# Expert adapters multiplied in the unused columns of the score banks, half of the products parked in DRAM

## The chip, the core and the metric

The kernel runs on one core of one Trainium2 chip. The metric is the device time of one execution in microseconds (us). The kernel before took 2158.56 us, the median of three runs (2157.76 to 2160.24). A difference is spoken of as such from 0.2% on.

## What is computed

Two transformer layers with normalisation after each block, over 8 batches of 512 tokens of width 512, all in float32. What matters here is the first layer: causal attention with 16 heads of 32, then a mixture of 8 experts of which each token uses two. Every expert's weights carry a low-rank adapter (rank R = 16, scale 2):

```python
gup = jnp.einsum('th,eho->teo', xf, gate_up_proj)
gup = gup + SCALING * jnp.einsum('ter,eor->teo', jnp.einsum('th,erh->ter', xf, gup_lora_A), gup_lora_B)
...
out = jnp.einsum('tei,eih->teh', h, down_proj)
out = out + SCALING * jnp.einsum('ter,ehr->teh', jnp.einsum('tei,eri->ter', h, down_lora_A), down_lora_B)
```

The kernel multiplies each adapter out once (A times B, a full 512 x 512 or 256 x 512 matrix) and adds it to the expert's weights, so that the tokens see merged weights. That is 8 experts x 6 chunks of 128 x 512.

## The kernel before

**Stages.** `attention0` (L1231) does the first attention for batches b = 0 to 7. Within a batch it goes over four groups of four heads, g = 0 to 3, and in each over three units u of score blocks (`UNITS`, L1239): u = 0 is key block 0, u = 1 is key blocks 1 and 3, u = 2 is key block 2, whose scores are 256 columns wide. The experts' tiles of 128 tokens follow (`Tiles.step`, L954), then the second attention and the feed-forward layer, which the change does not touch.

**A unit.** `scores` (L1392) takes the tile `sc`, four PSUM banks of 512 columns, one bank for each head of the group; the pool `p_sc` has one such buffer. Each score matmul is cut into two of 64 columns (`matmul_by_columns`, L58), and the four heads lie on four different groups of 32 rows, so that eight matmuls stand side by side in the array. ScalarE takes the exponential of all four banks (L1403), GpSimd masks the diagonal (L1408). For u = 2 only columns 0 to 255 of each bank are used. After the scores come the thunks that `plan(b)` (L1453) has put into the slot `todo[g, u]` (projections, queries, keys, values, routing), then the product of the unit before (L1413), and at u = 1 the row sums of the group before (L1434), whose inverse goes through the two `r_inv` buffers.

**The adapters.** `merge` (L1447) handles one chunk of two experts: two matmuls with 16 rows and 128 columns each into two buffers of the pool `p_mm` (which has two, and serves all projections), two multiplications by 2 on ScalarE into `r_inv` buffers (L800), two additions into the weights on GpSimd (L802). Twelve of the 24 merges lie in batches 1 to 6, two in each, in the slots (2, 2) and (3, 2) behind the batch's key or ahead of its `score`. The other twelve, for experts 4 to 7, come after the last attention group: their weights can be loaded only once the memory of the attention weights is free (`room`, L768). They are spread over `tiles.step` 0 to 10, one in each (L1552 to L1585). Tile 12 is the first that uses an expert from 4 on.

**Who sets the order.** Up to batch 7, g = 2, and for the other engines up to L1586, a scheduler orders each engine's instructions by its own estimate of times; from there on TensorE keeps the order of the source (`in_order`, L65, L1532). SyncE (SP) issues nearly all DMAs from one queue, in order: loads, the `results` of the tiles (L936), the normalised rows (L195). GpSimd (POOL) issues the gathers of token rows (L850) and does the two small operations of each layer normalisation (L189, L190), in one queue with its additions.

**Around the end of the attention.** Step 0 of the tiles, then batch 7's output projection (L1558 to L1562), whose four tiles VectorE adds and takes statistics of (L1336, L187, L188). GpSimd makes the reciprocal deviation (L189, L190), VectorE normalises (L192), and behind that in VectorE's queue lie the routing table (L597, L598) and the hidden product of the next tile (L913), which TensorE turns in `turn_hidden` (L919).

Of the kernel before, what the change touches and what calls it, by code (L numbers as in the profile page):

```python
# [9 lines left out]
F32 = mybir.dt.float32  # L10
# [4 lines left out]
ALU = mybir.AluOpType  # L15
# [3 lines left out]
P = 128  # L19
NB = 8  # L20
S = 512
# [3 lines left out]
E = 8  # L25
R = 16
NHID = 1408 // P
UPS = 6
# [3 lines left out]
LORA_SCALE = 2.0  # L32
# [14 lines left out]
EXPERT = UPS * 512  # L47
# [10 lines left out]
def matmul_by_columns(nc, out, lhsT, rhs, start=True, stop=True, columns=32):  # L58

    for at in range(0, P, columns):  # L60
        m = slice(at, at + columns)
        nc.tensor.matmul(out[m], lhsT=lhsT[:, m], rhs=rhs, start=start, stop=stop)  # L62
# [8 lines left out]
class Inputs:  # L71
# [3 lines left out]
    def __init__(self, *aps):  # L75
        for name, ap in zip(self.names, aps, strict=True):
            setattr(self, name, ap)
# [156 lines left out]
def lora_factors(lo, c):  # L234

    if c < ND:
        return lo[:, ts(c, P)], lo[:, 512:1024]
    return lo[:, 1536 + P * (c - ND) : 1536 + P * (c - ND + 1)], lo[:, 1024:1536]
# [520 lines left out]
class Experts:  # L759

    def __init__(self, env, pool):
        self.env, self.nc = env, env.nc
        self.w = pool.tile([P, E * EXPERT], F32, name="experts")
        self.by_expert = self.w.rearrange("p (e f) -> p e f", f=EXPERT)

# [15 lines left out]
        for j in range(4):  # L783
            self.nc.sync.dma_start(out=self.lora[32 * j : 32 * j + R, :], in_=self.env.ins.lora[i, j])

    def delta(self, ps, e, c):
        j = 32 * (e % 4)
        a, bt = lora_factors(self.lora[j : j + R, :], c)
        self.nc.tensor.matmul(ps, lhsT=a, rhs=bt, start=True, stop=True)

    def chunk(self, e, c, n=1):
        return self.by_expert[:, e : e + n, 512 * c : 512 * (c + 1)]

    def merge(self, e, c, ps, scaled):


        for i in range(2):
            self.delta(ps[i], e + i, c)
        for i in range(2):
            self.nc.scalar.mul(scaled[i], ps[i], LORA_SCALE)  # L800
            w = self.chunk(e + i, c)[:, 0, :]
            self.nc.gpsimd.tensor_tensor(w, w, scaled[i], ALU.add)  # L802


class Tiles:
# [425 lines left out]
def attention0(env, guard, keep, routes, experts, dram, p_mm, tiles_ctx):  # L1231
# [4 lines left out]
    tc, nc, ins, xs, vec = env.tc, env.nc, env.ins, env.xs, env.vec  # L1236
# [3 lines left out]
    with ExitStack() as phase:  # L1240
# [22 lines left out]
        def load_x(b):  # L1263
            xs[b] = work.tile([P, NT, D], F32, tag="x", name=f"x_{b}", bufs=2)
            nc.sync.dma_start(out=xs[b], in_=ins.x[b].rearrange("(t p) d -> p t d", p=P))
# [30 lines left out]
        def mm(shape, name):  # L1296
            return p_mm.tile(shape, F32, tag="mm", name=name)
# [94 lines left out]
        def scores(b, g, u):  # L1392
            q, k = heads[b, g]
            sc = p_sc.tile([P, 4, S], F32, tag="sc", name="sc")
            width = 0
            for kt in UNITS[u]:
                w = S - P * kt
                for j in range(4):
                    hs = slice(HD * j, HD * (j + 1))
                    matmul_by_columns(nc, sc[:, j, width : width + w], k[hs, ts(kt, P)], q[hs, P * kt :], columns=64)  # L1400
                width += w
            p = own.tile([P, 4, width], F32, tag=f"p{u}", name="p", bufs=2 if u == 0 else 1)
            nc.scalar.activation(p, sc[:, :, :width], AF.Exp, scale=scale)  # L1403

            at = 0
            for kt in UNITS[u]:
                first = p[:, :, at : at + P]
                nc.gpsimd.affine_select(out=first, in_=first, pattern=[[0, 4], [1, P]], compare_op=ALU.is_ge, fill=0.0,  # L1408
                                        base=0, channel_multiplier=-1)
                at += S - P * kt  # L1410
            return p
# [30 lines left out]
            nc.vector.tensor_tensor(aoTs[b][:, g, :], av, r_inv, ALU.mult)  # L1442
            guard.watch_inverses(r_inv)

        merges = [(e, c) for e in range(0, E, 2) for c in range(UPS)]

        def merge(n=1):  # L1447
            for _ in range(min(n, len(merges))):
                e, c = merges.pop(0)
                ps = [mm([P, 512], "ps_lora") for _ in range(2)]  # L1450
                experts.merge(e, c, ps, [work.tile([P, 512], F32, tag="r_inv", name="scaled", bufs=2) for _ in ps])

        def plan(b):  # L1453

            todo, late = ({(g, u): [] for g in range(ND) for u in range(len(UNITS))} for _ in range(2))
            for slot, places in (((0, 0), (0, 1)), ((0, 1), (3,)), ((0, 2), (2,))):
                todo[slot] += [lambda t=t: value(b, t) for t in places]
            pb, last = b - 1, b == NB - 1
            by_dma = 0 <= pb < by_blocks
            for g in range(ND):  # L1460
                nb, ng = (b, g + 1) if g + 1 < ND else (b + 1, 0)
                if nb < NB:
                    todo[g, 0 if by_dma and ng == 0 else 1].append(lambda nb=nb, ng=ng: query(nb, ng))
                    todo[g, 1 if by_dma and ng == 0 else 2].append(lambda nb=nb, ng=ng: key(nb, ng))
            if b:
                places = ((1, 0), (1, 1), (1, 2), (2, 0)) if by_dma else ((1, 0), (1, 0), (1, 1), (1, 1) if last else (1, 2))
                for t, slot in enumerate(places):
                    todo[slot].append(lambda t=t: project(pb, t))
                if by_dma:
                    todo[2, 1].append(lambda: blocks(pb))  # L1470
                else:
                    for c in range(ND):
                        at = todo[2, 1] if last and c >= 2 else (late if last else todo)[2, 0]
                        at.insert(c % 2 if at is todo[2, 1] else len(at), lambda c=c: turn(pb, c))
                todo[(3, 2) if by_dma else (2, 1)].append(lambda: score(pb))
                if not by_dma:
                    todo[2, 2].append(lambda: choose(pb))
                if not last:
                    todo[2, 2 if by_dma else 1].append(merge)
                    todo[3, 2 if by_dma else 1].insert(0, merge)  # L1480
            if b == 0:
                todo[1, 0].append(lambda: router.merge_lora(mm([P, ND, E], "ps_wr")))
            if b > 1:
                todo[0, 0].append(lambda: choose(b - 2))
                todo[1, 0].append(lambda: dispatch(b - 2))
                todo[1, 2].append(lambda: enter(one_hot(b - 2, range(NT))))
            if last:
                todo[1, 2].append(soon)
                todo[2, 2].append(first_rows)
                late[3, 1].append(first_turned)  # L1490
                todo[3, 2] += [begin, lambda: dispatch(b - 1)]
            return todo, late
# [25 lines left out]
        for b in range(NB):  # L1518
            todo, late = plan(b)
            for g in range(ND):  # L1520
                if g == 2:
                    if b + 1 < NB:
                        load_xT(b + 1)

                    nc.gpsimd.tensor_tensor(xs[b], xs[b], row[:, 1:2, :].to_broadcast([P, NT, D]), ALU.add)
                if g == 3 and b + 1 < NB:
                    load_x(b + 1)
                if b == NB - 1 and g == 1:
                    experts.load_lora(work, 1)
                    experts.load(4)  # L1530
                if b == NB - 1 and g == 2:
                    order.enter_context(in_order(tc))  # L1532
                if b == NB - 1 and g == 3:
                    experts.load(5)
                    experts.load(6)
                acc = []
                for u in range(len(UNITS)):
                    p = scores(b, g, u)
                    for thunk in todo[g, u]:
                        thunk()  # L1540
                    begun.close()
                    if waiting is not None:
                        waiting()
                    for thunk in late[g, u]:
                        thunk()
                    if u == 1 and summing is not None:
                        summing()
                    waiting = lambda b=b, g=g, u=u, p=p, acc=acc: product(b, g, u, p, acc)
                summing = lambda b=b, g=g, acc=acc: normalise(b, g, acc)
# [6 lines left out]
        b = NB - 1  # L1556
# [321 lines left out]
def usual_pass(tc, ins, held_out):  # L1878
    nc = tc.nc
    with ExitStack() as ctx:  # L1880
        env = Env(ctx, tc, ins)
# [3 lines left out]
        with tc.tile_pool(name="a_mm", bufs=2, space=PSUM) as p_mm, ExitStack() as attn1_ctx:  # L1885
            with tc.tile_pool(name="routes", bufs=1, side="right") as routes, \
                    tc.tile_pool(name="experts", bufs=1, side="right") as pool, ExitStack() as tiles_ctx:
                experts = Experts(env, pool)
                router, tiles, tables = attention0(env, guard, keep, routes, experts, dram, p_mm, tiles_ctx)

                def load_rows(b):
# [335 lines left out]
```

## Time and profile before

| what | us |
|---|---|
| median of three runs | 2158.56 |
| the profiled execution, its own time | 2158.07 |
| its span on the core | 2156.4 |
| outside the span (2158.07 less 2156.4) | 1.67 |
| TensorE busy | 2121.3 |
| window 148 to 235 (about one batch): TensorE, VectorE, ScalarE, GpSimd busy | 86.57, 60.76, 27.97, 29.84 |
| window 690 to 810 (end of the attention, first tiles): the same | 118.33, 62.34, 32.66, 50.69 |

TensorE's busy time counts matmuls from their start to a modelled end, and matmuls that overlap once. Since a 512-column matmul's modelled end lies past the start of the next, the price of a group of matmuls is best taken from start to start: the time from its first start to the start of the next group. In the timeline, the columns are the start in us, the duration, the engine, the source line, the operation with output, inputs, array tile (rows*columns) and operand shape, how many records are merged, and in brackets the idle time before with what ended it. A float32 matmul leaves two records.

### The profile page before, as it was taken

To read this page: it belongs to the slowest core of one execution; us is meant where nothing else is said; L and a number is where in the kernel's file an instruction comes from. 1 tells how busy PE (TensorE), PEld (TensorE's weight loads), DVE (VectorE), ACT (ScalarE), POOL (GpSimd) and SP (SyncE) were. 2 spreads that over 40 slices of the span, in tenths; PEclk is the share of its full clock that TensorE was granted. 3 is DMA by queue.
4 is the path that set the end of the run, shared out by engine and by line. 5 is a ranking of instruction groups with operands and counts; after the bars stand their busy time and mean duration, and the time that the engine had idled before them with its cause. 6 is when DMAs were issued, how large, how long until landed. Compare 5 with 4: busy or idle time off the path is not lost. (4 is left out here: it accounts for less than half of the span.)

```text
span 2156.4 us, 35260 instructions
## 1 busy us (share of the span) xinstructions
PE 2121.3 (98%) x14746; PEld 996.3 (46%) x14746; DVE 1280.0 (59%) x2042; ACT 628.8 (29%) x907; POOL 495.0 (23%) x489
## 2 busy tenths in 40 slices
PE   9999999999998999999999999999999999999997
PEld 2333333333333444444443333333334888888886
DVE  2657676776767544224326988889857644555443
ACT  2332323323323221122124333332332232222222
POOL 2333414424233342132014222232211000000000
PEclk9999999999999999999999999999999999999999
DMA  9030312303222228797644121331201311111000
GB/s 308 21 95 6 99 30 71 99 2 98 71 68 89 98 91 231 214 234 195 193 157 139 57 87 55 98 98 40 79 1 45 103 59 59 59 59 59 20 20 21
DMA packets 160010, 195.53 MB, mean 91 GB/s; under 512 B 61010, under 2 KB 101970, under 8 KB 157282
## 3 DMA queue, kind: packets, MB, share of 16 engines
q1 hardware_dynamic: 148560, 157.49, 23.8%
q0 software_dynamic: 10560, 34.61, 5.6%
q8 instruction: 119, 1.95, 0.4%
q10 hardware_dynamic: 722, 1.07, 0.1%
q14 instruction: 49, 0.40, 0.1%
HBM read 123.67 MB, written 69.47 MB: 90 GB/s over the span
## 5 line engine op out<-in xcount | busy, mean ns | idle before, releaser
L911 PE MATMUL ps_gu<-experts,xrT 128*128 128x512 f32 (+1 forms) x520 | 247.4, 598 | 0.0
L1403 ACT ACTIVATE p<-sc 128x2048 f32<-128x2048 f32 (+1 forms) x96 | 153.1, 1595 | 144.8 <-PE sc L62 121.1
L1165 DVE SCALAR_TENSOR_TENSOR hT<-ps_u,vec,sg 128x512 f32<-128x512 f32 x88 | 65.6, 746 | 189.4 <-PE ps_u L1160 189.4
L1176 PE MATMUL ps_f<-ffn_w,h_half 128*128 128x512 f32 x672 | 169.7, 393 | 2.7 <-DVE h_half L1171 2.0
L1015 POOL TENSOR_TENSOR g_total<-g_total,r_inv 128x512 f32<-128x512 f32 x64 | 90.0, 1406 | 352.4 <-DVE r_inv L1788 270.2
L1408 POOL TENSOR_SCALAR_AFFINE_SELECT p<-p 128x512 f32<-128x512 f32 x128 | 90.2, 717 | 341.0 <-ACT p L1403 303.5
L1431 DVE TENSOR_TENSOR p<-p 128x1536 f32<-128x1536 f32 (+2 forms) x96 | 139.3, 1451 | 44.6 <-POOL p L1408 41.2
L1758 ACT ACTIVATE p<-sc 128x1024 f32<-128x1024 f32 x128 | 124.1, 1022 | 99.0 <-PE sc L62 98.9
L913 DVE TENSOR_TENSOR h<-ps_gu,h 128x256 f32<-128x256 f32 x67 | 28.5, 425 | 207.0 <-ACT h L912 207.0
L1788 DVE RECIPROCAL r_inv<-r_inv 128x512 f32<-128x512 f32 x32 | 107.1, 3346 | 68.5 <-ACT r_inv L1012 68.5
L1176 PEld LDWEIGHTS ps_f<-ffn_w,h_half 128*128 128x128 f32 x672 | 124.4, 188 | 34.9 <-DVE h_half L1171 7.7
L1160 PE MATMUL ps_g<-x_high,ffn_w 128*128 128x512 f32 x352 | 137.2, 390 | 0.9 <-DVE x L1730 0.9
L1160 PE MATMUL ps_g<-x_low,ffn_w 128*128 128x512 f32 x352 | 137.0, 389 | 0.0
L911 PEld LDWEIGHTS ps_gu<-experts,xrT 128*128 128x128 f32 x520 | 95.6, 196 | 89.5 <-issue 89.2
L1160 PE MATMUL ps_u<-x_high,ffn_w 128*128 128x512 f32 x352 | 136.9, 389 | 0.0
L1160 PE MATMUL ps_u<-x_low,ffn_w 128*128 128x512 f32 x352 | 136.9, 389 | 0.0
L927 PE MATMUL ps_y<-experts,hT 128*128 128x512 f32 (+1 forms) x272 | 128.0, 593 | 0.5 <-ACT hT L921 0.5
L62 PE MATMUL ps_q<-experts 128*32 128x512 f32 x1024 | 121.9, 605 | 4.9 <-DMA experts<-in_xT 4.6
L62 PE MATMUL sc<-qT,kT 64*64 64x512 f32 x1024 | 124.7, 602 | 1.1 <-ACT qT L1664 0.7
L1777 PE MATMUL av<-p,v 128*64 128x512 f32 x512 | 120.9, 593 | 0.0
L62 PE MATMUL ps_o<-attn_out,aoT 128*64 128x512 f32 x512 | 116.4, 598 | 0.8 <-ACT r_inv L1012 0.8
L62 PE MATMUL ps_k<-experts 128*32 128x512 f32 x1024 | 116.3, 594 | 0.0
(269 smaller groups left out, 3275.8 us busy)
## 6 DMA issues: line engine op xcount, KB each, us to landing
results<-y SPq DMA_DIRECT2D x68, 256.0 KB, 2.2
turned<-turned SPq DMA_DIRECT2D x56, 256.0 KB, 4.1
pair<-xrT SPq DMA_DIRECT2D x25, 512.0 KB, 3.1
xrT<-pair SPq DMA_DIRECT2D x100, 128.0 KB, 4.5
x<-in_x SPq DMA_DIRECT2D x8, 1024.0 KB, 8.3
experts<-in_gate_up SPq DMA_DIRECT2D x8, 1024.0 KB, 11.4
rows<-x SPq DMA_DIRECT2D x32, 256.0 KB, 2.3
x<-rows SPq DMA_DIRECT2D x8, 1024.0 KB, 15.4
```

The source lines that it names most:

```text
L62: nc.tensor.matmul(out[m], lhsT=lhsT[:, m], rhs=rhs, start=start, stop=stop)
L911: nc.tensor.matmul(ps, lhsT=xT[:, c, :], rhs=self.weights(i, c), start=c == 0, stop=c == ND - 1)
L927: self.nc.tensor.matmul(ps, lhsT=hT[:, c, :], rhs=self.weights(i, ND + c), start=c == 0, stop=c == self.NI - 1)
L1015: self.nc.gpsimd.tensor_tensor(self.total, self.total, r_inv, ALU.add)
L1160: nc.tensor.matmul(ps, lhsT=w[:, ts(dc, P)], rhs=x[:, dc, :], start=(dc, i) == (0, 0), stop=(dc, i) == (ND - 1, 1))
L1176: self.nc.tensor.matmul(os[t], lhsT=h[:, ts(t, P)], rhs=self.weights(2 * NHID + c), start=(c, i) == (0, 0), stop=(c, i) == (NHID - 1, 1))
L1403: nc.scalar.activation(p, sc[:, :, :width], AF.Exp, scale=scale)
L1408: nc.gpsimd.affine_select(out=first, in_=first, pattern=[[0, 4], [1, P]], compare_op=ALU.is_ge, fill=0.0, base=0, channel_multiplier=-1)
L1431: nc.vector.tensor_tensor(total[:, :, P * kt :], total[:, :, P * kt :], p[:, :, at : at + w], ALU.add)
L1758: nc.scalar.activation(p, sc, AF.Exp, scale=scale)
L1777: nc.tensor.matmul(st["av"][HD * j : HD * (j + 1), :], lhsT=st["v"][:, kt, HD * j : HD * (j + 1)], rhs=p[:, j, :], start=kt == 0, stop=kt ...
L1788: nc.vector.reciprocal(r_inv, r_inv)
```

## The change

- `merge` in batches 1 to 6 and its matmuls in the tail are gone. In their place, each unit u = 2 of batches 1 to 6 (24 units) computes half a chunk, 256 columns, for four experts at once, in the free columns 256 to 511 of its own `sc` banks (`delta_halves`): four adapters on four row groups, each cut in two by 64 columns, ahead of the unit's scores.
- After the unit's exponential, ScalarE multiplies two banks at a time by 2 into two new buffers `scaled0`, `scaled1` (one of each), two multiplications in each unit (`merge_halves`).
- In batches 1 to 3 these are experts 0 to 3, and GpSimd adds them to the weights. In batches 4 to 6 they are experts 4 to 7, and SP writes them to a DRAM tensor `deltas`.
- In the tail `merge` reads the products back into the `r_inv` buffers (24 reads of 256 KB on SP) and GpSimd adds them. Its twelve places stay, without matmul and ScalarE work.
- The second set of adapters is loaded in batch 4 rather than in batch 7.
- The scratch area of GpSimd's DMA descriptors is halved (8192 bytes per partition[...]), which makes room for the two buffers.

```diff
@@ Experts
-    def __init__(self, env, pool):
+    def __init__(self, env, pool, dram):
         self.env, self.nc = env, env.nc
+        self.deltas = dram.tile([P, 4, EXPERT], F32, name="deltas")
...
-    def delta(self, ps, e, c):
-        j = 32 * (e % 4)
-        a, bt = lora_factors(self.lora[j : j + R, :], c)
-        self.nc.tensor.matmul(ps, lhsT=a, rhs=bt, start=True, stop=True)
-
-    def chunk(self, e, c, n=1):
-        return self.by_expert[:, e : e + n, 512 * c : 512 * (c + 1)]
-
-    def merge(self, e, c, ps, scaled):
-
+    def delta_halves(self, ps, c, half):
+
+        for e in range(4):
+            a, bt = lora_factors(self.lora[32 * e : 32 * e + R, :], c)
+            matmul_by_columns(self.nc, ps[:, e, :], a, bt[:, 256 * half : 256 * (half + 1)], columns=64)
+
+    def merge_halves(self, ps, second, c, half, scaled):
+
+        f = slice(512 * c + 256 * half, 512 * c + 256 * (half + 1))
+        for e, two in zip((0, 2), scaled):
+            two = two.rearrange("p (e f) -> p e f", e=2)
+            self.nc.scalar.mul(two, ps[:, e : e + 2, :], LORA_SCALE)
+            if second:
+                self.nc.sync.dma_start(out=self.deltas[:, e : e + 2, f], in_=two)
+            else:
+                w = self.by_expert[:, e : e + 2, f]
+                self.nc.gpsimd.tensor_tensor(w, w, two, ALU.add)
+
+    def merge(self, e, c, deltas):
 
         for i in range(2):
-            self.delta(ps[i], e + i, c)
-        for i in range(2):
-            self.nc.scalar.mul(scaled[i], ps[i], LORA_SCALE)
-            w = self.chunk(e + i, c)[:, 0, :]
-            self.nc.gpsimd.tensor_tensor(w, w, scaled[i], ALU.add)
+            self.nc.sync.dma_start(out=deltas[i], in_=self.deltas[:, e + i - 4, ts(c, 512)])
+            w = self.by_expert[:, e + i, ts(c, 512)]
+            self.nc.gpsimd.tensor_tensor(w, w, deltas[i], ALU.add)
@@ attention0, scores(b, g, u)
             sc = p_sc.tile([P, 4, S], F32, tag="sc", name="sc")
+            beside = halves.pop(0) if u == 2 and 0 < b < NB - 1 else None
+            if beside:
+                experts.delta_halves(sc[:, :, S - 256 :], *beside[1:])
...
             nc.scalar.activation(p, sc[:, :, :width], AF.Exp, scale=scale)
+            if beside:
+                scaled = [own.tile([P, 512], F32, tag=f"scaled{i}", name="scaled") for i in range(2)]
+                experts.merge_halves(sc[:, :, S - 256 :], *beside, scaled)
...
-        merges = [(e, c) for e in range(0, E, 2) for c in range(UPS)]
+        halves = [(second, c, half) for second in (False, True) for c in range(UPS) for half in range(2)]
+        merges = [(e, c) for e in range(4, E, 2) for c in range(UPS)]
 
         def merge(n=1):
             for _ in range(min(n, len(merges))):
                 e, c = merges.pop(0)
-                ps = [mm([P, 512], "ps_lora") for _ in range(2)]
-                experts.merge(e, c, ps, [work.tile([P, 512], F32, tag="r_inv", name="scaled", bufs=2) for _ in ps])
+                experts.merge(e, c, [work.tile([P, 512], F32, tag="r_inv", name="delta", bufs=2) for _ in range(2)])
@@ plan(b)
-                if not last:
-                    todo[2, 2 if by_dma else 1].append(merge)
-                    todo[3, 2 if by_dma else 1].insert(0, merge)
@@ the loop over b and g
+                if b == NB // 2 and g == 0:
+                    experts.load_lora(work, 1)
                 if b == NB - 1 and g == 1:
-                    experts.load_lora(work, 1)
                     experts.load(4)
@@ kernel
-    nc = bacc.Bacc("TRN2", target_bir_lowering=False, num_devices=1)
+    nc = bacc.Bacc("TRN2", target_bir_lowering=False, num_devices=1, dynamic_dma_scratch_size=8192)
```

More of the change, by code (lines that the diff above doesn't have):

```diff
@@ L1887, in usual_pass @@
                     tc.tile_pool(name="experts", bufs=1, side="right") as pool, ExitStack() as tiles_ctx:
-                experts = Experts(env, pool)
+                experts = Experts(env, pool, dram)
                 router, tiles, tables = attention0(env, guard, keep, routes, experts, dram, p_mm, tiles_ctx)
```

## The prediction

> **What bounds the kernel now.** I read the page's first part, then the timeline of TensorE in one batch and at the end of the attention, then GpSimd's and VectorE's timelines there, last the DMA issues. The first line of the page says that TensorE is the bound:
>
> ```profile
> PE 2121.3 (98%) x14746; PEld 996.3 (46%) x14746; DVE 1280.0 (59%) x2042; ACT 628.8 (29%) x907; POOL 495.0 (23%) x489
> ```
>
> So matmul time that goes is gained, unless TensorE then waits. TensorE in batch 2 (groups g = 2 and g = 3), an adapter pair amid the work:
>
> ```profile
> 231.66 3.64 PE L62 MATMUL ps_k<-experts 128*32 128x512 f32 x32
> 235.23 2.00 PE L789 MATMUL ps_lora<-lora 16*128 16x512 f32 x4
> 237.16 1.07 PE L1423 MATMUL av<-p,v 128*32 128x384 f32 x16
> ...
> 249.54 0.69 PE L62 MATMUL sc<-q,k 32*64 32x256 f32 x16
> 250.16 1.44 PE L789 MATMUL ps_lora<-lora 16*128 16x512 f32 x4
> 252.03 1.06 PE L498 MATMUL ps_logits<-x1T,r_wr 128*32 128x512 f32 x8 [0.43 <-ACT scaled L800]
> ```
>
> From start to start the first pair costs 237.16 - 235.23 = 1.93 us, the second 252.03 - 250.16 = 1.87. At the end of the attention the same pair costs less, since both `p_mm` buffers are free:
>
> ```profile
> 726.84 1.13 PE L789 MATMUL ps_lora<-lora 16*128 16x512 f32 x4
> 727.90 1.98 PE L911 MATMUL ps_gu<-experts,xrT 128*128 128x512 f32 x4
> 729.72 0.38 PE L919 MATMUL ps_hT<-ident,h 128*128 128x128 f32 x2
> ```
>
> That is 1.06 us; the batches pay about 0.85 more for waiting on a buffer. GpSimd and VectorE at the same place, where batch 7 is normalised and the next tile's hidden product follows:
>
> ```profile
> 721.12 0.23 POOL L189 TENSOR_SCALAR rstd<-mv 128x4 f32<-128x4 f32 x1 [12.40 <-DVE mv L188]
> 721.43 1.04 POOL L190 TENSOR_TENSOR rstd<-rstd,neg_half 128x4 f32<-128x4 f32 x1
> ```
> ```profile
> 722.52 1.92 DVE L192 TENSOR_SCALAR x<-x,mv,rstd 128x512 f32<-128x512 f32 x4 [1.49 <-POOL rstd L190]
> ...
> 725.21 0.42 DVE L913 TENSOR_TENSOR h<-ps_gu,h 128x256 f32<-128x256 f32 x1
> ```
>
> The reader is to see a chain: from the start of `rstd` to the end of `h` 725.63 - 721.12 = 4.5 us, and TensorE turns that `h` at 729.72, four us later.
>
> [...]eight-tile groups of 512 columns go from 219.66 to 220.70, 1.04 us, and groups of 384 and 128 one behind the other from 199.51 to 200.56, 1.05. The fixed part is paid once for groups of the same mode. [...]The trace has 2.2 for writes of that size and, for loads issued by SP with 2 KB rows, 4.3 at 512 KB.
>
> **Part 1, batches 1 to 6.** Removed: in every batch one pair of 1.93 and one of 1.87, that is 3.80. Added: four half chunks. 256 columns at the rate of a projection wave (200.56 to 204.01, 3.45 us for four waves of 512, so 0.86 each) are 0.43, and the fixed part of 0.18 is shared with the scores of the same mode that follow. Bounds: 0.43 and the stand-alone price of a 256-column group, 250.16 - 249.54 = 0.62. I take 0.43; four are 1.72.
>
> Added wait: the next group's scores need the one `sc` buffer, now free only after two more multiplications (1.08 for two, from 728.06 in ScalarE's timeline; 0.6 for one). Behind them on TensorE stands everything. For g = 0, 1 and 2 a key (3.5) and a product (1.0) lie between, which hide it; the exponential of u = 2 ends at 232.85 and the next scores start at 238.16. Without the pair those would start at 236.2, and the key's copy on ScalarE ends at 236.05, so nothing is left but also nothing lost. For g = 3 only `score` (0.88) and a product (1.0) lie between: `sc` starts at 249.97, the exponential runs from about 250.7 to 251.8, the multiplications to 252.85, the next scores could start at 253.0, TensorE would be there at 252.4. The order of the built programs shows that the scheduler puts one lone value matmul there and takes it out of the following batch of four: 0.86 for a wave of its own. Bounds 0 and 0.86; I take 0.86.
>
> Per batch -3.80 + 1.72 + 0.86 = -1.22, times six **-7.3 us** (bounds: -12.5 with the lone matmul free, -2.8 with halves at 0.62).
>
> Beside it, priced at nothing: ScalarE has eight multiplications in a batch rather than four, 2.4 us more on 28 busy of 87; GpSimd eight additions (1.5 on average) rather than four in batches 1 to 3, none in 4 to 6, on 30 of 87; SP has eight writes of 256 KB in a batch, which stand ahead of the rows and loads in its queue, but wait for ScalarE only at the end of u = 2, long before those are due. If ScalarE had no slack at g = 3, each multiplication would cost 0.6. The adapters' four loads, moved from batch 7 to SP's queue in batch 4, have two units of scores and products and three values (3.5 each) until their first use, some 15 us against the 7.4 that such a load takes to land. The halved scratch: gathers are issued 1.26 us apart and land in 4.0, so about four are in flight; nothing shows that half the room is too little. Zero; the upper bound is a gather that waits for the one before, and at 4 us each the gathers of the tiles would still keep pace with a step of 5.95.
>
> **Part 2, the tail.** Removed: twelve pairs. From start to start in TensorE's timeline: 1.99 (696.30), 1.06 (702.14), 1.06, 1.06 plus a wait of 0.15 (733.90), 1.06 of 1.87 at 744.09 (the rest waits for the logits' copy, which stays), and seven of 1.06. The sum is **13.8**. A step then takes 5.95 rather than 7.06.
>
> Added: the additions wait for reads from DRAM. In the built order GpSimd's queue is now: four gathers, addition 1, a gather, the last `g_total`, additions 2 to 12, and only then `rstd` of batch 7. Before, four additions stood ahead of it. So the normalisation waits for twelve reads, which pass through two buffers. The times, on the clock of before: the gathers start at 696.67 as now and end at 701.5; addition 1 (1.27) ends at 702.8 and frees its buffer; read 2 lands L later. From then on each buffer goes read, addition, read: L + 1.27 + 0.2 for the semaphores. Addition 2 ends at 704.3 + L, addition 4 at 705.8 + 2L, addition 12 four cycles later, at 711.7 + 6L. That is when `rstd` starts. Its input would be there at 718, so this wait is the last. The hidden product ends 4.5 us later, TensorE can turn it 0.1 after that. TensorE would be there at 729.72 - 1.99 - 1.06 - 1.06 = 725.6. The stall is 711.7 + 6L + 4.6 - 725.6 = **6L - 9.3**.
>
> L is not in the trace. Below: the 2.2 of the writes. Above: 4.3, the median of the 512 KB loads. Gathers of 256 KB take 3.5 to 4.2 with the issue on GpSimd (about 1 us) in it. I take 3.2: stall 9.9. At 2.2 it is 3.9, at 4.3 it is 16.5.
>
> What waits behind: three gathers behind additions 16, 22 and 24, not needed before steps 6 to 9, some 20 us later; expert 7's load and `results` behind the reads on SP, with two output buffers, about even with their need by the same arithmetic, 0 to 2 us; I take 0. The tail nets -13.8 + 9.9 = **-3.9**.
>
> **Sum.** -7.3 - 3.9 = -11.2, against the execution's own 2158.07 (span 2156.4 and 1.67 around it): **2146.9**. The median of the runs is 0.49 above the profiled one, nothing that matters here.
>
> **The rivals.** (a) Reads as quick as writes: the stall is 3.9 and the time 2140.9, or 2136 with the lone matmul free as well. For it: hardly any traffic at that place. Against it: no load on SP's queue has a median below 3.6 in the list of DMA issues. (b) No change: reads at 3.9 (stall 14.1, tail +0.3) and halves at 0.62 each (-2.8): 2155.6. For it: the 512 KB loads; half a chunk takes sixteen weight loads where a pair took four. (c) Slower, by one mechanism: the chain of reads and additions ahead of `rstd`. The gain is eaten at 6L - 9.3 = 7.3 + 13.8, L = 5.1; at L = 6 the stall is 26.7 and the time 2163.7. For it: loads of 256 KB at the kernel's start, amid other traffic, take 3.6 to 4.0, and five gathers and an expert's load run beside these. Against it: the DMA share in that window is 0.28. (d) That the change doesn't do what it says cannot be: the built order has all 24 groups in their places.
>
> **How the numbers follow.** Forecast 0.51 (2143 to 2152), (a) 0.22, (b) 0.16, (c) 0.11. What a measurement of this kernel can tell from no change is 0.2%, 4.3 us. Faster are the forecast and (a), 0.73; the same 0.16; slower 0.11. The range reaches from (a), 2137.5, to past (b), 2157; what is left out is (c) and a little of (a).
>
> **What would show it.** Right: groups of `sc` out of `lora` at 0.4 us each; batches 1 to 6 each 1.2 us shorter; batch 7's `rstd` idle on a DMA or on additions until about 731; a wait of TensorE for `h` of about 10 us near 726, and none later. Wrong: an L outside 2.2 to 4.3; a wait of `sc` for ScalarE in g = 0 to 2; TensorE waiting for gathers or outputs at later steps; halves at over 0.62.

## The result and the profile after

The changed kernel takes 2164.4 us (median of 10 runs, 2160.9 to 2168.0), the kernel before 2158.6 in the same comparison; the ratio is 1.0027, 95% interval 1.0018 to 1.0035. So it is slower by about 6 us, where 2146.9 was forecast. The profiled execution spans 2162.6 us against 2156.4. The page's first part shows what kind of loss that is:

```profile
PE 2106.2 (97%) x15034; PEld 995.6 (46%) x15034; DVE 1280.4 (59%) x2042; ACT 627.7 (29%) x907; POOL 488.4 (23%) x489
```

TensorE is busy 15.1 us less than before (2121.3), as the change meant it to be, and still ends 6.2 later: it now waits 21 us more, that is, stands idle for something that isn't there yet. The waits of TensorE in the kernel after (engine, operation, line, what it waited for; us in total, times, longest) name new ones (`x1T` are the turned rows that come back from DRAM for the router, `p` the masked scores, `av` their product with the values):

```profile
PE ps_logits L498 <- DMA x1T<-turned: 5.4, 3, 2.6
PE ps_rank L62 <- DVE xrT L895: 4.4, 1, 4.4
...
PE av L1437 <- POOL p L1422: 3.9, 3, 1.7
PE ps_o L1338 <- DVE x L1344: 2.7, 1, 2.7
...
PE ps_hT L927 <- DVE h L921: 2.6, 1, 2.6
```

Only the last was in the forecast. To place the loss I use two marks in TensorE's timeline that every kernel here has: the start of the last group of row sums `rs` (before: 695.30), and the stretch from it to the 67th of the 68 groups of `ps_y` that follow (before: 413.2). Up to the first mark the changed kernel loses 5.6 us (forecast -7.3); between the marks it gains 0.3 (forecast -3.9); behind them it loses 0.9.

The end of batch 2 in TensorE's timeline of the kernel after, which answers to the pair shown of before:

```profile
248.13 0.69 PE L62 MATMUL sc<-lora 16*64 16x256 f32 x16
248.61 0.64 PE L62 MATMUL sc<-q,k 32*64 32x256 f32 x16
249.18 1.07 PE L498 MATMUL ps_logits<-x1T,r_wr 128*32 128x512 f32 x8
...
251.21 1.02 PE L62 MATMUL ps_v<-experts 128*32 128x512 f32 x2
```

The half chunk and the scores together take 249.18 - 248.13 = 1.05, where the scores alone took 0.62: the half costs 0.43, as priced. The last line is the lone value matmul (a group of values that stands by itself). The batches' ends (starts of `ps_logits`) lie at 162.88, 249.18 and 335.52, before at 165.40, 252.03 and 338.56: 2.5 to 3.0 us ahead. Then it turns. Batch 4 ends at 424.62, batch 5 at 512.96, batch 6 at 602.85 (before 425.32, 513.10, 599.73), so that a lead of 3.0 has become a lag of 3.1. SyncE's timeline at the end of batch 4, first before, then after:

```profile
410.33 1.24 SPq L1265 DMA_DIRECT2D x<-in_x  x1
```
```profile
410.65 2.94 SPq L800 DMA_DIRECT2D deltas<-scaled  x2
413.69 0.46 SPq L1273 DMA_DIRECT2D x<-in_x  x1
415.01 0.33 SPq L103 DMA_DIRECT2D x1T<-turned  x1
```

Two writes of group g = 2 stand ahead of the load of `x`. On GpSimd the addition to `x` then starts late (first before, then after), with the masks of `p` behind it; on TensorE, `ps_logits` waits for `x1T` and `av` for the mask:

```profile
419.71 4.55 POOL L1525 TENSOR_TENSOR x<-x,row 128x2048 f32<-128x2048 f32 x1 [2.25 <-DMA x<-in_x]
```
```profile
422.20 4.51 POOL L1536 TENSOR_TENSOR x<-x,row 128x2048 f32<-128x2048 f32 x1 [7.74 <-DMA x1T<-turned]
```
```profile
424.62 1.07 PE L498 MATMUL ps_logits<-x1T,r_wr 128*32 128x512 f32 x8 [1.94 <-DMA x1T<-turned]
427.36 1.07 PE L1437 MATMUL av<-p,v 128*32 128x384 f32 x16 [1.67 <-POOL p L1422]
```

The table of windows says why (window, its length, busy time and instructions of TensorE, its weight loads, VectorE, ScalarE and GpSimd, then the granted clock as a share of full speed, the busy share of the DMA engines, and GB/s). Here 420 to 424, before and after:

```profile
420.00:424.00 4.00, 4.00 (x47) 1.40 (x40) 0.00 (x0) 1.66 (x4) 4.00 (x1) 1.00 0.63 242
```
```profile
420.00:424.00 4.00, 2.68 (x48) 0.85 (x40) 0.00 (x0) 2.57 (x5) 1.80 (x1) 1.00 1.00 398
```

From 408 to 420 the share was 0.91 to 0.96 already before. The mean over window 148 to 235, 0.20, hid such a stretch of some 15 us with the DMA engines nearly always busy. Before, it ends at about 422.5 (a share of 0.63 of the four us); the changed TensorE is at `ps_logits` at 424.62 - 1.94 = 422.7, so there was next to no slack for two writes more.

The third such wait, 2.58 us at 602.85, costs more than it lasts. The windows behind it show the granted clock, 0.50 in the second:

```profile
600.00:603.00 3.00, 0.42 (x20) 0.18 (x8) 0.00 (x0) 2.00 (x3) 3.00 (x1) 1.00 0.39 148
603.00:606.00 3.00, 3.00 (x24) 1.04 (x18) 1.90 (x1) 0.58 (x1) 1.65 (x3) 0.50 0.46 159
```

In finer windows the half clock lasts from 603.0 to 606.2, so 1.6 us are lost. (The kernel before has such stretches too, 682.2 to 685.7 and 747.0 to 750.4.) In the tail, the places that the forecast showed of before (GpSimd, VectorE, TensorE):

```profile
730.85 1.27 POOL L810 TENSOR_TENSOR experts<-experts,delta 128x512 f32<-128x512 f32 x1 [0.61 <-DMA delta<-deltas]
732.09 0.23 POOL L189 TENSOR_SCALAR rstd<-mv 128x4 f32<-128x4 f32 x1
```
```profile
733.49 1.92 DVE L192 TENSOR_SCALAR x<-x,mv,rstd 128x512 f32<-128x512 f32 x4 [7.08 <-POOL rstd L190]
```
```profile
736.58 0.69 PE L927 MATMUL ps_hT<-ident,h 128*128 128x128 f32 x2 [2.57 <-DVE h L921]
737.06 3.12 PE L919 MATMUL ps_gu<-experts,xrT 128*128 128x512 f32 x4
```

`rstd` starts as the twelfth addition ends, `h` is late, and behind the wait the next group takes 3.12 rather than 1.88: half clock again (0.50 from 736.2 to 739.5).

### The profile page after: what moved, and what is told of

It is laid out like the page before. It is cut to its first block, busy times and chain, and to the rows that moved or that the text cites. A ratio compares the mean times of both kernels' runs of the same rounds, so it can differ in the third digit from the quotient of the medians.

```text
span 2162.6 us, 35888 instructions
## 1 busy us (share of the span) xinstructions
PE 2106.2 (97%) x15034; PEld 995.6 (46%) x15034; DVE 1280.4 (59%) x2042; ACT 627.7 (29%) x907; POOL 488.4 (23%) x489
## 5 line engine op out<-in xcount | busy, mean ns | idle before, releaser
L1422 POOL TENSOR_SCALAR_AFFINE_SELECT p<-p 128x512 f32<-128x512 f32 x128 | 81.9, 653 | 200.1 <-ACT p L1414 196.6
L62 PE MATMUL ps_v<-experts 128*32 128x512 f32 x1024 | 121.1, 595 | 0.0
```

## The experiments

All were timed beside the kernel before, which took 2157.9 to 2159.0 in these comparisons. "Attention" is the first mark less that of before, "tail" the stretch between the marks less that of before, both from the profile of one execution. Where the tail's program is that of before it reads 0.0 to 1.7: half clock costs 1.7 us between the marks in the kernel before and in the first set only, 3.4 in the three runs that read 1.6 or 1.7. The attention of the four kernels with the writes behind the loads and four halves in each of the batches 1 to 6 is the same program, and reads -2.6 to -4.5. And the profiled execution can lie off the median of its runs (writes by ScalarE 2.9 above, both mends 2.3 above, first set only 2.3 below). So 2 us in these two columns mean little; the ratios rest on 5 to 19 runs each.

| run | us | ratio to before [95%] | attention | tail |
|---|---|---|---|---|
| the change | 2164.4 | 1.0027 [1.0018, 1.0035] | +5.6 | -0.3 |
| first set only | 2152.1 | 0.9974 [0.9965, 0.9984] | -9.7 | 0.0 |
| writes behind loads | 2154.1 | 0.9980 [0.9973, 0.9986] | -3.0 | -1.1 |
| writes by ScalarE | 2162.2 | 1.0018 [1.0010, 1.0025] | +7.6 | -1.7 |
| no round trip | 2140.3 | 0.9921 [0.9907, 0.9934] | -3.7 | -14.0 |
| no additions | 2139.9 | 0.9922 [0.9909, 0.9934] | -4.5 | -14.0 |
| GpSimd in order | 2158.5 | 1.0002 [0.9993, 1.0010] | +4.4 | -4.2 |
| both mends | 2149.5 | 0.9961 [0.9948, 0.9974] | -2.6 | -2.9 |
| scratch alone | 2157.3 | 0.9994 [0.9986, 1.0002] | -0.6 | 1.7 |
| first set, none at g = 3 | 2145.4 | 0.9943 [0.9930, 0.9957] | -15.1 | 1.7 |
| before, no tail additions | 2158.2 | 1.0002 [0.9994, 1.0010] | -0.9 | 1.6 |
| all, one at g = 3 | 2151.6 | 0.9976 [0.9968, 0.9984] | -1.9 | -6.2 |
| clear of routing | 2148.3 | 0.9952 [0.9938, 0.9965] | -2.8 | -7.6 |

**First set only.** The tail's `merge` is that of before, with matmuls and ScalarE, and the second adapters load in batch 7 again.

```diff
-            beside = halves.pop(0) if u == 2 and 0 < b < NB - 1 else None
+            beside = halves.pop(0) if u == 2 and 0 < b < NB // 2 else None
```

> One part of the change alone: experts 0 to 3 are multiplied out in the score banks in batches 1 to 3; the twelve pairs of experts 4 to 7 stay in the tail as matmuls, as before, and nothing goes through DRAM. Batches 4 to 6 then carry neither pairs nor halves. My theory (the loss of the change sits in the round trip through DRAM: writes in batches 4 to 6, reads in the tail): the attention loses 6 x 3.80 us of pairs, gains 12 halves of 0.45 and, in the three batches with halves, about 1.8 us at the start of the following batch, so -22.8 + 5.4 + 5.5 = -12; the tail is as before; 2146.5 us, between 2143 and 2151. Rival (the halves themselves, their ScalarE work and the order of GpSimd's queue cost what the pairs did): within 4 us of before, 2155 or more. Second rival (the halved scratch area slows the gathers): the tail is longer than before by several us, whatever the attention does.

Measured 2152.1, one over the range and below the rival's 2155: without DRAM the change gains. The attention gives 9.7 of the expected 12; batches 4 to 6, which have no pairs, now end on the mask (`av` waits 3.5 us for it there).

**Writes behind loads.**

```diff
-                self.nc.sync.dma_start(out=self.deltas[:, e : e + 2, f], in_=two)
+                write = lambda out=out, two=two: self.nc.sync.dma_start(out=out, in_=two)
+                write() if held is None else held.append(write)
...
+            while beside and held:
+                held.pop(0)()
```

> The changed kernel with one difference: in batches 4 to 6 the two writes of group g = 2 are issued by SP behind the load of x and the return of x1T, not ahead of them. My theory (these two writes, 2.9 us of SP's time, hold up the load of x and the return of x1T; TensorE then waits for x1T at the score and for the mask that stands behind the addition to x on GpSimd): the three waits for x1T (1.94, 0.90, 2.58 us) and most of the waits for the mask (1.67, 1.54) go, with the half clock that follows the longest (1.6); 8 to 10 us less than the changed kernel, 2155 us. Rival (it is the traffic of the writes as a whole or ScalarE's work that slows batches 4 to 6): no more than 2 us less, 2162 or more.

Measured 2154.1, 10.4 less than the change. The place of six writes, two in each of three batches, is worth 8.6 us of attention. GpSimd and TensorE at the end of batch 4 in this run:

```profile
418.84 4.56 POOL L1541 TENSOR_TENSOR x<-x,row 128x2048 f32<-128x2048 f32 x1 [4.08 <-DMA x<-in_x]
```
```profile
422.93 1.06 PE L498 MATMUL ps_logits<-x1T,r_wr 128*32 128x512 f32 x8
```

**Writes by ScalarE.**

```diff
-                self.nc.sync.dma_start(out=self.deltas[:, e : e + 2, f], in_=two)
+                self.nc.scalar.dma_start(out=self.deltas[:, e : e + 2, f], in_=two)
```

> The changed kernel with all 24 writes issued by ScalarE, at the same points of the program, so that SP's queue is as before the change and the traffic is that of the change. If SP's time for issuing is the cause (2.9 us ahead of the loads), nearly all of the 8 to 10 us comes back, less what ScalarE loses by issuing (each issue delays the logits' copy or the next exponential): 2156 to 2159. If the cause is that 512 KB of writes share the DMA engines with the loads of x, x1T and xT (3 MB), the waits for x1T stay at 1 us or more and no more than 4 us come back: 2160 to 2164.

Measured 2162.2, in the range that stood for the traffic: SyncE's 2.9 us of issuing are not the cause, and that part of my theory falls. SyncE issues the load of `x` ahead of where it did in the change (411.85 rather than 413.69), and the addition to `x` is as late as there:

```profile
422.62 4.51 POOL L1536 TENSOR_TENSOR x<-x,row 128x2048 f32<-128x2048 f32 x1 [8.41 <-DMA x1T<-turned]
```

So it made no difference to that addition which engine issued the 512 KB: it starts at 422.62, against 422.20 with SyncE's writes and 419.71 before. The DMA engines are as busy, with a share of 0.95 to 1.01 in every two us from 410 to 424.

**No round trip, and no additions.** The first leaves out writes, reads and additions. The second, on the kernel with the writes behind the loads, keeps writes and reads:

```diff
-            w = self.by_expert[:, e + i, ts(c, 512)]
-            self.nc.gpsimd.tensor_tensor(w, w, deltas[i], ALU.add)
```

> The changed kernel with the products of experts 4 to 7 computed and scaled as in the change, but neither written to DRAM nor read back nor added: the adapters of experts 4 to 7 are left out of the result. It prices the whole round trip with the twenty-four additions in the tail. My theory: attention shorter than before by about 1.3 us per batch at most (-12.4 of pairs against halves, +5.7 of lone value matmuls, +2 to +4 of waits for the value's copy): -3 to -5; tail shorter by the pairs' 13.8 less what VectorE cannot keep up with (2.7 at the output projection, 2 to 4 at the routing): -7 to -9; together 2145 to 2149. Rival (the halves and the freed tail are worth nothing even without DRAM, since VectorE and the order of the queues take it all): 2154 or more.

> The kernel with the two writes behind the loads (2154.1 us), with the products of experts 4 to 7 written and read back, but the 24 additions on GpSimd in the tail left out: the adapters of experts 4 to 7 are missing from the result. It tells the reads on SP's queue from the additions on GpSimd. My theory (the tail loses to the additions: the normalisation stands behind twelve of them, and VectorE's short operations last until a GpSimd addition beside them is over, 1.2 us where 0.2 to 0.3 are usual): the tail becomes that of the kernel without the round trip, 13 us less, 2141 us, between 2139 and 2144, and the waits of TensorE for VectorE at the output projection (3.3) and at the ranks (4.5) are gone. Rival (24 reads of 256 KB ahead of the outputs in SP's queue hold two output buffers and with them VectorE): these waits stay, 2148 or more.

Measured 2140.3 and 2139.9, the first below its range. In both the tail is shorter by 14.0, about what the pairs had cost (13.8; in part by chance, since TensorE also waits 3.5 us there, where before shows 0.2, and loses 1.7 less to half clock). So 24 reads that wait for no addition cost nothing, VectorE keeps up (I had it losing 5 to 7), and the 24 additions cost as much as the pairs. How, VectorE's and GpSimd's timelines of the change show, during the routing of batch 7:

```profile
757.21 1.27 DVE L534 SCALAR_TENSOR_TENSOR rest<-r_hots,pr 128x32 f32<-128x32 f32 x1
...
758.74 1.25 DVE L526 TENSOR_TENSOR tmp<-rest,second 128x32 f32<-128x32 f32 x1
```
```profile
757.17 1.26 POOL L810 TENSOR_TENSOR experts<-experts,delta 128x512 f32<-128x512 f32 x1 [1.16 <-DMA delta<-deltas]
758.67 1.27 POOL L810 TENSOR_TENSOR experts<-experts,delta 128x512 f32<-128x512 f32 x1 [0.24 <-DMA delta<-deltas]
```

and the same two operations without additions:

```profile
739.14 0.19 DVE L534 SCALAR_TENSOR_TENSOR rest<-r_hots,pr 128x32 f32<-128x32 f32 x1
...
739.58 0.19 DVE L526 TENSOR_TENSOR tmp<-rest,second 128x32 f32<-128x32 f32 x1
```

Each of these operations meets an addition and ends with it: the first at 758.48, its addition at 758.43, the second at 759.99, its addition at 759.94. Not every operation is held so. The reciprocal at 754.92 lies inside an addition (754.74 to 756.01) and keeps its 0.18, while the product at 755.14 lasts 0.92, to 756.06 (0.19 without additions). The rival, that the reads in SyncE's queue hold up the tiles' outputs and with them VectorE, does not fit the trace: from 754.92 to the copy that TensorE waits for (763.51) VectorE has no idle time, and between the marks it waits for an output only once, at 1077.85.

TensorE at the ranks, before, in the change with the group behind it at half clock, and without additions:

```profile
755.61 0.41 PE L62 MATMUL ps_rank<-both,r_before 128*128 128x32 f32 x2
```
```profile
764.25 0.63 PE L62 MATMUL ps_rank<-both,r_before 128*128 128x32 f32 x2 [4.39 <-DVE xrT L895]
...
765.12 3.76 PE L919 MATMUL ps_gu<-experts,xrT 128*128 128x512 f32 x4
```
```profile
743.47 0.41 PE L62 MATMUL ps_rank<-both,r_before 128*128 128x32 f32 x2 [0.94 <-DVE xrT L895]
```

**GpSimd in order, and both mends.** GpSimd keeps the program's order in the tail; the second run has the writes behind the loads as well.

```diff
         waiting()
         summing()
+        pinned = phase.enter_context(ExitStack())
+        pinned.enter_context(in_order(tc, mybir.EngineType.Pool))
         merge()
...
+        pinned.close()
         order.close()
```

> The changed kernel with GpSimd's tail kept in the order of the program from the last attention group on: four additions, not twelve, stand ahead of the reciprocal deviation of batch 7, and two additions follow in each step. My theory (the normalisation behind twelve additions costs the stall of 2.6 us at the hidden product and the half clock after it, 1.2; the other waits come from additions beside VectorE's work and stay): 3 to 5 us less than the changed kernel, 2160.5, between 2158 and 2163. Rival (the stall only moves: VectorE is the bound from the output projection on): no change, 2163.5 or more.

> Both mends together: the two writes of g = 2 behind the loads, and GpSimd's tail in the order of the program. If the two are independent: 2154.1 less 1.3 for the stall that is left there at the hidden product and what the half clock costs, 2151.5, between 2149 and 2153.5. If GpSimd's order only moves the wait: 2154 or more.

Measured 2158.5 (5.9 less than the change, within the range, though its 14 runs spread from 2154.1 to 2165.2) and 2149.5. `rstd` starts as its input arrives (idle before it 10.97, for `mv`), and the wait for `h` is gone. TensorE's waits for `x` at the output projection (1.9) and ahead of the ranks (4.8 and 5.3) stay. The run without additions shows no wait at the first place and 0.94 at the second, so I put them down to additions beside VectorE's operations.

**Scratch alone.** On the kernel before.

```diff
-    nc = bacc.Bacc("TRN2", target_bir_lowering=False, num_devices=1)
+    nc = bacc.Bacc("TRN2", target_bir_lowering=False, num_devices=1, dynamic_dma_scratch_size=8192)
```

> The kernel before with the scratch area for GpSimd's DMA descriptors halved and nothing else. My theory: no effect, 2158.4 within 1 us. Rival (gathers wait for room): more than 1 us slower.

Measured 2157.3 against 2158.3: it costs nothing that these runs could show.

**First set, none at g = 3.**

```diff
-            beside = halves.pop(0) if u == 2 and 0 < b < NB // 2 else None
+            beside = halves.pop(0) if u == 2 and g < 3 and 0 < b < 5 else None
```

> Experts 0 to 3 in the score banks as in the run with the first set only (2152.1 us), but the twelve half chunks lie in g = 0, 1 and 2 of batches 1 to 4 and none in g = 3; the pairs of experts 4 to 7 stay in the tail, nothing goes through DRAM. The built order has no lone value matmul any more. My theory (a half chunk at g = 3 costs, besides its 0.45, a value matmul of its own at 0.95 and a wait of 0.7 for the value's copy at the start of the next batch): three times 1.65 is gone, 2147, between 2144.5 and 2149.5. Rival (what TensorE saves there it waits for elsewhere, since the mask behind the addition to x ends the batch): no more than 2 us less, 2150 or more.

Measured 2145.4, 6.7 less than with three of them at g = 3, where 5 was expected, and the best of all: 12.5 us under before, 19 under the change.

**Before, no tail additions.** On the kernel before, in `merge`.

```diff
             self.nc.scalar.mul(scaled[i], ps[i], LORA_SCALE)
+            if e >= 4:
+                continue
             w = self.chunk(e + i, c)[:, 0, :]
             self.nc.gpsimd.tensor_tensor(w, w, scaled[i], ALU.add)
```

> The kernel before with the 24 additions of experts 4 to 7 in the tail left out (their matmuls and multiplications stay): these adapters are missing from the result. It asks whether the additions, which cost 14 us in the changed tail, cost something in the tail of before. My theory (VectorE waits for a GpSimd addition beside it there too, but TensorE with its pairs is the slower, except around the routing of batch 7): 0 to 2 us less than before, 2157. Rival (the additions on GpSimd are a cost of this tail at any pace): 5 us less or more, 2153 or below.

Measured 2158.2 against 2157.9: there the same additions are free. My reason, that TensorE with its pairs is slower than VectorE with its collisions, is not shown by this run. A VectorE operation beside an addition is long there too (`mine<-r_part,r_hots` at 756.84 lasts 0.93, to 757.77, where it takes 0.18 without additions), but in the trace of before the additions hardly meet the routing at all: they lie at 745.99 to 748.47 and from 756.44 on, and the two operations shown above take 0.19 each, at 750.03 and 750.48. So the place of the additions may count as much as the pace of TensorE.

**All, one at g = 3.** From both mends; writes held back go out at the next u = 2.

```diff
-            beside = halves.pop(0) if u == 2 and 0 < b < NB - 1 else None
+            at_unit = (g in (1, 2)) if b == 0 else (g < 3 or b == 6)
+            beside = halves.pop(0) if u == 2 and at_unit else None
```

> The kernel with both mends (2149.5 us) and the 24 half chunks spread over g = 1 and 2 of batch 0, g = 0 to 2 of batches 1 to 7 and one g = 3 in batch 6, so that only one lone value matmul is left. By the same theory five lone value matmuls of 0.95 and three waits of 0.7 for the value's copy go: 7 us less, 2143, if nothing else waits; the halves in batch 7 and the last write stand close to the tail's first read, which may give 1 or 2 us back: between 2142 and 2147. Rival (the mask and the loads at the batch's end take it): 2148 or more.

Measured 2151.6, a miss. From batch 1's end to batch 7's (`ps_logits` at 169.56 and 666.98, in both mends 163.83 and 667.10) it gains the expected 5.9. In the profile batch 0 takes it back: two additions (57.43 to 59.9) stand there ahead of a mask for which TensorE waits, with half clock behind it (a mean granted clock of 0.66 from 60 to 65):

```profile
60.56 1.07 PE L1442 MATMUL av<-p,v 128*32 128x256 f32 x8 [3.87 <-POOL p L1427]
```

In the sum the attention is as long as with both mends. The profiled execution lies 2.2 below the median of its runs, and why that median is 2.1 above both mends stays open; the two intervals overlap.

**Clear of routing.** From both mends; no merges in the three steps of the routing, two in each of the last steps.

```diff
         choose(b, P)
         tiles.step()
-        merge()
...
             tiles.step()
-            merge()
+            merge(2)
```

> The kernel with both mends (2149.5 us) and one more difference: the three merges that lay in the steps of batch 7's routing are taken out of those steps and done two at a time in the steps after them, so that no addition of GpSimd lies beside VectorE's routing chain. My theory ([...]the copy of the next token rows, queued behind the routing, comes late): TensorE's wait before the ranks falls from 4.8 to about 1 us, as in the kernel without additions, and the half clock after it (3 us more for the two groups that follow) goes: 6 to 7 us less, 2143, between 2141 and 2146. Rival (the wait before the ranks comes from the outputs behind the reads in SP's queue, or the weights of experts 4 to 7 now come late): no more than 2 us less, 2147.5 or more.

Measured 2148.3: 1.2 less than both mends by the medians, 1.9 by the ratios, which is the size that the rival gave. Its reason isn't what shows, though: the wait ahead of the ranks falls from 4.79 to 0.94, and the second routing table comes 7.0 us earlier (70.06 rather than 77.05 after the first mark). Of that, 4.8 are left at the second mark: with two merges to a step the additions stand ahead of gathers, for which TensorE waits at two steps (0.31, 0.75). Another 1.5 go behind the second mark, which I did not settle, and the profiled execution of both mends lies 2.3 above the median of its runs: 4.8 - 1.5 - 2.3 is 1.0, about the 1.2 of the medians.

## Why the prediction was wrong

The likeliest case and the rivals (a) and (b) were wrong; (c) came near the time (2163.7) by a mechanism that is not the one at work: its L was 6, and L is 2.45. That is luck. Of the 17.5 us between forecast and result some 12.9 lie in the attention (-7.3 against +5.6), 3.6 in the tail (-3.9 against -0.3), 0.9 behind.

**Right.** Halves at 0.43. The lone value matmul at 0.95 (priced 0.86). The removed pairs of the tail at 13.8 (14.0 when nothing takes their place, in part by chance). Zero for the scratch area. The chain through `rstd`: additions 2 and 12 start at 711.24 and 730.85, so two take 3.92, which leaves 3.92 - 1.27 = 2.65 from the end of an addition to the next one on its buffer. The read is issued 0.03 after that end (712.52 and 712.55); my 0.2 for the semaphores is an assumption that no run shows by itself, and with it L is 2.45; the formula's 711.7 + 6L gives 726.4, and `rstd` starts at 732.09 less the 5.62 by which the attention is late, 726.47. Only the size of L was off, 3.2 against 2.45; the stall by the formula is 5.4. TensorE shows 2.57 of it, because the wait for `x` ahead of it (2.74) makes TensorE itself late.

**Wrong, the step that decided.** "SP has eight writes of 256 KB in a batch, which stand ahead of the rows and loads in its queue, but wait for ScalarE only at the end of u = 2, long before those are due", priced at nothing. It asked when the loads are needed and not how busy the DMA engines were ahead of that (a share of 0.91 to 0.96 from 408 to 420). It is worth 8.6 us of attention by the marks; by the waits it is 9.4, for `x1T` (5.4) and for the mask (3.9, of which 1.5 stay with the writes behind the loads), with half clock after the longest (1.6). With that mended the attention gains 3.0 of the 7.3.

**Wrong, the rest of part 1.** At the start of batches 2 to 4 TensorE waits 0.7 for the value's copy (2.1 in all): on GpSimd the mask stands behind the sum that waits for `r_inv`, and an addition lies beside VectorE's product (2.30 us at 171.59, 1.71 before), so the copy comes late. Half chunks at g = 3 cost more than the 0.86 that I priced: 5.4 us of attention for three of them, 1.8 each (6.7 by the medians). From 7.3 to 3.0 are 4.3: 2.1 for these waits, 1.5 for the mask, 0.5 for six lone matmuls at 0.95. That makes 4.1, but the same attention reads up to 1.9 us apart from profile to profile, so no run shows this split.

**Wrong, part 2.** "The tail nets -13.8 + 9.9" counted one stall; the additions on GpSimd make TensorE wait at three places. Against the run without additions, after the last row sums:

| point | before | the change | no additions |
|---|---|---|---|
| first routing table | 23.89 | 23.65 | 20.65 |
| first `ps_x1T` | 39.66 | 42.36 | 35.12 |
| ranks | 60.31 | 63.33 | 52.64 |
| second routing table | 74.88 | 79.56 | 65.91 |

The change falls behind by 3.0 up to the first table (wait for `x`, 2.74: VectorE's one-hot operations beside GpSimd's additions, 1.92 at 708.89, 1.25 at 711.32 and at 715.34, where the medians of the same operations are 0.31 and 0.25), by 4.2 to `ps_x1T` (the foreseen stall, 2.57, and half clock), by 3.5 to the ranks (4.39 less the 0.94 that stay), by 3.0 to the second table (half clock after that wait, 763.5 to 770.2): 13.7. Part 2 noted no effect of GpSimd on VectorE. My price of 9.9 was nearer to the sum than to its own term, by accident. That `results` behind the reads cost 0 was right: TensorE has no wait for them between the marks.

## What to carry to other kernels

Before adding DMAs, read the DMA share in the few microseconds ahead of each load that something waits for, not over the stage, and put writes that nobody waits for behind such loads. Additions on GpSimd are not free beside VectorE even when both have slack on average: the 24 that cost nothing in the tail of before cost 14 us in the changed one, where they lie beside other operations of VectorE and TensorE has less of its own work. And doing a change by halves pays: the part without DRAM was the gain, the other ate it.

## What the runs showed of the hardware

- After waits of 2.57 to 2.64 us TensorE was granted half clock for about 3 us (603.0 to 606.2 in the change), after 4.39 for 6.7 us (763.5 to 770.2); after 1.94 at 424.62, and after 2.74 at 717.60, it was not. The length of the wait doesn't decide it alone. The same wait at the same place of the program brought half clock in the kernel before (a granted clock of 0.52 from 682.2 to 685.7) and none with both mends (1.00 from 675 to 690):

```profile
681.18 1.19 PE L62 MATMUL sc<-q,k 32*64 32x384 f32 x32 [2.48 <-ACT p L1403]
```
```profile
679.33 1.12 PE L62 MATMUL sc<-q,k 32*64 32x384 f32 x32 [2.48 <-ACT p L1416]
```

  And before has half clock from 747.0 to 750.4, where the longest wait near it is 0.8 us (1.87 less 1.06, at 744.09). What does decide it, these runs don't show. A stretch of 3.2 us at a granted clock of 0.50 costs 1.6 us where TensorE is busy all through (an estimate, 3.2 x 0.50); later waits can absorb part of it (from these two lines to the first mark it is 14.12 us with half clock and 13.37 without).
- Beside a GpSimd addition of 1.26 us, two VectorE operations that take 0.19 without additions (`rest<-r_hots,pr`, `tmp<-rest,second`) took 1.27 and 1.25. Inside such additions the reciprocal `red<-red` kept its 0.18 (754.92) and `tmp<-ps_r,red` its 0.19 (754.22). The one-hot operations, with medians of 0.25 to 0.31, took up to 1.92. What separates the operations that last until the addition's end from those that don't, these runs don't show.
- Of reads of 256 KB from DRAM, issued each as its buffer came free, the addition that used one started 2.65 us after its buffer was free; the list of DMA issues of the run without additions has a median of 3.0 for them and 2.4 for the writes, and the list of before 2.2 for writes of 256 KB (`results<-y`).
- Score matmuls of 32x64 tiles ran side by side: in before the 16 records of `sc` from 219.66 on last 0.59 to 0.64 us each and start within 0.5 us of each other, and the next group starts 1.04 us after the first of them. Groups of 384 and 128 columns one behind the other take 1.05 (199.51 to 200.56); a projection's wave of 512 takes 0.86 (3.45 for four from 200.56 on).
